# Inner v of a graph layer: two tiles of nodes by seven products in place of eight, and its bias added behind the attention weights

## The chip, the cores and the metric

The kernel runs on one core of a Trainium2 chip. TensorE (PE in the profile) multiplies matrices and writes PSUM; VectorE (DVE) and ScalarE (ACT) do the elementwise work and empty PSUM; GpSimd (POOL) and SyncE (SP) mostly start DMAs. The metric is the device time of one execution in microseconds.

## The reference

The input has 384 nodes of 1024 features. A layernorm is followed by a graph attention layer with 16 heads of 64, then a feed-forward network with fake quantisation, each with a residual. What matters here, with n the normalised input:

```
q, k, v = n @ wq.T + bq, n @ wk.T + bk, n @ wv.T + bv
q2, k2, v2 = q @ wiq.T + biq, k @ wik.T + bik, v @ wiv.T + biv   # "inner" projections
scores = q2 @ k2.T / 8 + mask                                    # per head, 384 x 384
out = softmax(scores) @ v2                                       # per head
x = x + out @ wo.T + bo
```

Everything in the attention layer is float32. The rows of a softmax sum to one, so a bias added to every row of v2 comes out of `softmax(scores) @ v2` unchanged.

## The kernel before, in words

The kernel goes through stages: the input's layernorm, the first projections q, k, v and inner q (22 to 159 us of the profiled span), the attention loop (159 to about 320), and the output projection with the feed-forward network.

The first projections and inner k already use a scheme of seven products in place of eight: two blocks of outputs by two halves of the columns, with sums of weights (`left_sums`, L171 to L175) and sums of activations (`right_sums`) made ahead on VectorE. `project2` runs the seven products, each four f32 matmuls of 128x128 by 192 columns (L191), and combines them while they are read out of PSUM: L205 and L215 on ScalarE, L202, L208, L219, L220 and L223 on VectorE; L212 makes one more weight sum in place.

The attention loop runs over p = 0 to 7, two heads at a time. Each p issues on TensorE: the scores of its two heads (`scores`, L639: first two tiles of rows, then the third); the transposes of the weights of p-1 (`weigh`, L669) and, at the end of p, their product with v2 (L677); some transposes for the quantised feed-forward weights (`prep`, L558, L568); and a filler, cut in sixteenths by `fill_to`, that keeps TensorE at work between these. The filler is inner k for the next two p (`project2`, at odd p) or a quarter of inner v (`inner_v(p // 2)`, at even p): 256 columns of v2 for all three tiles of nodes, each tile by eight matmuls of 256 columns (L613), emptied by one VectorE addition that adds the bias row (L619). At p = 7 the filler is the output projection (L687). Inner k and inner v write their PSUM tiles in the pool `ps_mm`, which holds two ("mm").

VectorE's part of one p: six score evictions (L645, scale, mask and row minimum), the reciprocals of the sums of exponentials (L657), six multiplications of the weights (L659), the copy of the product with v2 into `outT` (L681), the evictions of the filler, and the quantisation of one or two rows of feed-forward weights (`quantise_rows`: L515, L516, L518, L527). ScalarE takes the exponentials (L649), the copies of the transposed weights (L671) and the rest of the quantisation (L521).

The order on TensorE, SyncE and GpSimd is the order of the program, written out by hand. In the attention loop VectorE's and ScalarE's order is left to the scheduler of the framework at compile time. `tc.issue_after(ins)` adds to what a block issues on the engine of `ins` that it stands behind `ins`; `taken[-1]` is the score eviction written last so far.

All loads go through SyncE's queue in program order: the weight tiles `wt` (512 KB each, eight buffers used in turn), and the rows of the feed-forward weights (`row`, three buffers). The small inputs, among them the biases, come through GpSimd's queue at the start.

Of the kernel before, what the change touches and what calls it, by code (L numbers as in the profile page):

```python
# [12 lines left out]


# [2 lines left out]

# [6 lines left out]
F32 = mybir.dt.float32  # L24
# [4 lines left out]
ALU = mybir.AluOpType  # L29
# [3 lines left out]
P = 128  # L33
N = 384
NT = N // P
F = 1024
KC = F // P
E = 6528
EC = E // P
# [4 lines left out]
HK = KC // 2  # L44
# [13 lines left out]
def row_bcast(ap, n):  # L58
    return bass.AP(tensor=ap.tensor, offset=ap.offset, ap=[[0, P], [1, n]])
# [3 lines left out]
def gnn_ffn_kernel(ctx: ExitStack, tc: tile.TileContext, a: dict, out: bass.AP):  # L63
    nc = tc.nc

    const = ctx.enter_context(tc.tile_pool(name="const", bufs=1))
    small = ctx.enter_context(tc.tile_pool(name="small", bufs=2))
# [4 lines left out]
    ps_mm = ctx.enter_context(tc.tile_pool(name="ps_mm", bufs=2, space=PSUM))  # L72
# [11 lines left out]
    x = act.tile([P, NT, F], F32, name="actT")  # L84
    for t in range(NT):
        if t == NT - 1:
            wq_first = [load_w("wq", o) for o in range(FIRST)]
        nc.sync.dma_start(x[:, t, :], a["x"][t * P : (t + 1) * P, :])
    bias_rows = const.tile([5 * KC, P], F32)
    etw = const.tile([P, 4], F32)  # L90
    clip = const.tile([P, 2], F32)
    biv_b = const.tile([P, F], F32)


    ident = const.tile([P, P], F32)
# [2 lines left out]
    ph1_stack = ExitStack()  # L98
    ph1 = ph1_stack.enter_context(tc.tile_pool(name="ph1", bufs=2))
    edges_i = ph1.tile([EC, 3, P], I32, name="edges_i", bufs=1)  # L100
    nc.gpsimd.dma_start(bias_rows, a["biases"])
    nc.gpsimd.dma_start(etw, row_bcast(a["L0_gnn_edge_type_weights"], 4))
    nc.gpsimd.dma_start(clip[:, 0:1], row_bcast(a["L0_ffn_clip_x"], 1))
    nc.gpsimd.dma_start(clip[:, 1:2], row_bcast(a["L0_ffn_clip_down"], 1))
# [37 lines left out]

    ident_b = const.tile([P, P], BF16)
    later = ph1.tile([P, GROUP * P], F32, name="later", bufs=1)
    bias = const.tile([P, 5 * KC], F32)
    w8 = const.tile([P, 4], F32)

    def right_sums(src, pool, name, in_place=True):
# [98 lines left out]
    vT = act.tile([P, KC, N], F32, name="actT")  # L247
    with ph1_stack:
# [65 lines left out]
        pt = ps_tp.tile([P, P], F32, name="tp")  # L314
# [37 lines left out]
        wln = small.tile([P, 4], F32, name="wln")  # L352
        nc.scalar.activation(wln, wexp, AF.Ln, bias=1.0)
        pt = ps_tp.tile([P, 512], F32, name="tp")
        nc.tensor.transpose(pt[:, : 5 * KC], bias_rows, ident[: 5 * KC, : 5 * KC])
        wq_next = [load_w("wq", o) for o in (2, 3)]
        sums_next, steps = left_sums(*wq_next, ph1)
        run(steps)
        nc.vector.tensor_copy(bias, pt[:, : 5 * KC])
        x_right, steps = right_sums(xnT, ph1, "x_right", in_place=False)  # L360
        run(steps)
        q_first(0, 2)
# [2 lines left out]
        pt = ps_tp.tile([P, 3, EC], F32, name="tp")  # L365
# [7 lines left out]
        def tables():  # L373

            wpos = small.tile([P, 4], F32, name="wpos")
            nc.vector.tensor_scalar(wpos, etw, 0.0, None, op0=ALU.max)
            nc.vector.tensor_copy(ident_b, ident)
            nc.vector.tensor_scalar(later, ahead, 0.0, None, op0=ALU.is_gt)
            yield

            ty = small.tile([P, EC], F32, name="ty")
            nc.vector.tensor_scalar(ty, ed[:, 2, :], -1.0, None, op0=ALU.add)
            wrap = small.tile([P, EC], F32, name="wrap")
            nc.vector.tensor_scalar(wrap, ty, 0.0, 4.0, op0=ALU.is_lt, op1=ALU.mult)
            yield
            ty1 = small.tile([P, EC], F32, name="ty1")
            nc.vector.tensor_add(ty1, ty, wrap)
            ty2 = small.tile([P, EC], F32, name="ty2")
            nc.vector.tensor_scalar(ty2, ty1, 0.0, 3.0, op0=ALU.max, op1=ALU.min)
            yield  # L390
            off = small.tile([P, P], F32, name="off")
            nc.vector.tensor_scalar(off, ident, 0.0, NO_EDGE, op0=ALU.is_equal, op1=ALU.mult)
            wsp = small.tile([P, 4], F32, name="wsp")
            nc.vector.tensor_add(wsp, wpos, wln)
            nc.vector.tensor_scalar(w8, wsp, 1.0 / SCALE, None, op0=ALU.mult)
            yield

            for t in range(NT):
                nc.vector.scalar_tensor_tensor(
                    mask[:, t, t * P : (t + 1) * P], ident, w8[:, 3:4], off, op0=ALU.mult, op1=ALU.add  # L400
                )
            yield
            nc.gpsimd.dma_start(mask_d.rearrange("(t p m) a -> p t (m a)", t=NT, p=P), mask)

            nc.vector.tensor_scalar(value, ty2, 0.0, w8[:, 0:1], op0=ALU.is_equal, op1=ALU.mult)
            for k in range(1, 4):
                vk = small.tile([P, EC], F32, name="vk")
                nc.vector.tensor_scalar(vk, ty2, float(k), w8[:, k : k + 1], op0=ALU.is_equal, op1=ALU.mult)
                nc.vector.tensor_add(value, value, vk)
                yield  # L410
# [57 lines left out]
        for i, (name, o) in enumerate(todo[:-1]):  # L468
            (wa, wb), sums = wq_next, sums_next
            right, dst, cols = work[name]  # L470
# [8 lines left out]
            sums_next, steps = left_sums(*wq_next, turned if todo[i + 1][0] == "wik" else ph1)  # L479
# [3 lines left out]
            if name == "wv" and o >= KC - 4:  # L483
                steps = in_turn(steps, islice(q_steps, 4))
            if name == "wiq" and o == KC - 4:
                k_right, k_steps = right_sums(kT, turned, "k_right")
                steps = in_turn(steps, islice(k_steps, 4))
# [22 lines left out]
    v2 = act.tile([P, NT, F], F32, name="actT")  # L510
    outT = act.tile([P, KC, N], F32, name="actT")
# [60 lines left out]
    prep = ffn_weights()  # L572

    next(prep)
    nc.sync.dma_start(biv_b, row_bcast(a["L0_gnn_biv"], F))

    with ExitStack() as ph:
        at = ph.enter_context(tc.tile_pool(name="at", bufs=4))
        pair_p = ph.enter_context(tc.tile_pool(name="pair", bufs=2))
        ps_sc = ph.enter_context(tc.tile_pool(name="ps_sc", bufs=4, space=PSUM))  # L580

        def inner_k(p):
# [11 lines left out]
                ps_mm, "mm",  # L594
            )

        def inner_v(c):

            cs = slice(c * 256, (c + 1) * 256)
            wt = []  # L600
            for j in range(2):
                wt.append(w.tile([P, F], F32, name="wt"))
                nc.sync.dma_start(
                    wt[j].rearrange("p (k o) -> p k o", k=HK),
                    a["wiv"][j * HK : (j + 1) * HK, :, cs].rearrange("k p o -> p k o"),
                )

            def steps():
                for t in range(NT):
                    pm = ps_mm.tile([P, 256], F32, name="mm")  # L610
                    for k in range(KC):
                        k0 = k % HK * 256
                        nc.tensor.matmul(  # L613
                            pm, vT[:, k, t * P : (t + 1) * P], wt[k // HK][:, k0 : k0 + 256],
                            start=(k == 0), stop=(k == KC - 1),
                        )
                        if k < KC - 1:
                            yield
                    nc.vector.tensor_add(v2[:, t, cs], pm, biv_b[:, cs])  # L619
                    yield  # L620

            return steps()


        taken = []
# [36 lines left out]
        def weigh(p, e):  # L662

            eT = [[None] * NT for _ in range(2)]
            for m in range(NT):
                for h in range(2):
                    pt = ps_tp.tile([P, N], F32, name="tp")
                    for t in range(NT):
                        nc.tensor.transpose(pt[:, t * P : (t + 1) * P], e[h][:, t, m * P : (m + 1) * P], ident)  # L669
                    eT[h][m] = at.tile([P, N], F32, name="eTs", bufs=6)  # L670
                    nc.scalar.copy(eT[h][m], pt)  # L671
                yield
            pav = ps_sc.tile([P, N], F32, name="sc")
            for m in range(NT):
                for h in range(2):
                    c0 = (2 * p + h) * D
                    nc.tensor.matmul(  # L677
                        pav[h * D : (h + 1) * D, :], v2[:, m, c0 : c0 + D], eT[h][m],
                        start=(m == 0), stop=(m == NT - 1),
                    )  # L680
            nc.vector.tensor_copy(outT[:, p, :], pav)  # L681
            yield

        def out_group(wo, t, g, ks, pm):
# [12 lines left out]
        NP = H // 2  # L697
# [4 lines left out]
        for p in range(NP):  # L702
# [4 lines left out]
            if p == NP - 1:  # L707
                early = [(t, g, ps_mm.tile([P, 512], F32, name="mm")) for t, g in ((0, 0), (0, 1))]
                fill, n = (s for t, g, pm in early for s in out_group(wo, t, g, range(NP - 2), pm)), 2 * (NP - 2)
            elif p % 2:  # L710
                k2_next, fill = inner_k(p + 1)
                n = 7 * HK + 1
            else:
                fill, n = inner_v(p // 2), NT * KC
            if p == NP - 2:

                x = act.tile([P, NT, F], F32, name="actT")
# [126 lines left out]
        for t in range(NT):  # L844
# [7 lines left out]
            for g, (c0, width) in enumerate(groups):  # L852
                pm = open_groups.get((t, g)) if t < NT - 1 else None
                ks = [NP - 1]
                if pm is None:
                    pool, name = (ps_mm, "mm") if g < 2 else (ps_sc, "sc")
                    pm, ks = pool.tile([P, 512], F32, name=name), range(KC)
                for k in ks:
                    nc.tensor.matmul(
                        pm[:, :width], outT[:, k, t * P : (t + 1) * P], wo[k][:, c0 : c0 + width],  # L860
                        start=(k == 0), stop=(k == KC - 1),
# [9 lines left out]
    with ExitStack() as ph:  # L871
# [85 lines left out]
        for col, ic, c0, width in ((0, 0, 0, N), (1, 1, 0, N), (2, 2, 0, N // 2), (3, 2, N // 2, N // 2)):  # L957
            i0, rows = ICS[ic]
            cs = slice(c0, c0 + width)
# [118 lines left out]
```

## Time and profile before

| | |
|---|---|
| median of 3 runs | 369.69 us (369.19 to 370.16) |
| profiled execution | 369.01 us, its span 367.2 us |
| granted TensorE clock | 0.996 |
| TensorE busy | 355.4 us (97%) |
| VectorE busy | 255.4 us (70%) |
| ScalarE busy | 116.1 us (32%) |
| GpSimd busy | 73.7 us (20%) |
| HBM | 41.91 MB read, 2.21 MB written |

How the profile is read: busy times are of one execution. An f32 matmul leaves two records on TensorE; the duration of one record is longer than its distance to the next, since matmuls are pipelined, so what one costs is read from a run of them in the chain. In lines of the timeline the columns are the start (us from the start of the span), the duration, the engine, the line of the kernel, the operation, output and inputs, their shapes, and how many were merged; a bracket names the idle time before it and what ended it. In the chain in order of time the columns are start, duration and what ran. In the table by stretches they are the stretch, its length, and then for each of TensorE, its weight loads, VectorE, ScalarE and GpSimd the busy time and the number of instructions; the last three are the granted clock, the DMA share and GB/s, and an engine without work may be left out of the line as it is quoted from a view of one engine.

### The profile page before, as it was taken

Reading aid. Unit: us, or ns where it says so; the run is one execution under the profiler, and the core shown is the slowest. Engines: PE = TensorE matmul, PEld = TensorE weight load, DVE = VectorE, ACT = ScalarE, POOL = GpSimd, SP = SyncE. Lnnn points to the kernel's source line nnn. Section 1 sums busy time; section 2 is a strip of 40 time slices with the busy share of each in tenths; the row PEclk is TensorE's granted clock in tenths of the full one; section 3 lists DMA queues with packets and bytes.
Section 4 is the critical chain, followed back from the end, with each engine's and each line's share of the span. In section 5 each row is a group of like instructions: output and inputs, shape, how many; then the busy total and the mean of one; then the engine's idle time right before and its main releaser. Section 6 shows DMA issues by size and latency. Waiting matters only on the chain.

```text
span 367.2 us, 5815 instructions
## 1 busy us (share of the span) xinstructions
PE 355.4 (97%) x2094; PEld 297.4 (81%) x2094; DVE 255.4 (70%) x786; ACT 116.1 (32%) x270; POOL 73.7 (20%) x81
## 2 busy tenths in 40 slices
PE   8999999999999999999999999999999999999981
PEld 7999999999999999998877879686867445449660
DVE  5788888888889989967286855747494521099775
ACT  2252000000000003214473737454553523133730
POOL 7010354455444543340000000000000000000003
PEclk9999999999999999999999999999999999999998
DMA  7969433343333367720500620031694000000004
GB/s 230 396 218 401 151 116 114 118 136 116 114 114 117 114 203 253 222 64 2 157 20 2 207 63 20 17 139 44 206 404 160 29 0 2 0 0 1 2 1 171
DMA packets 17804, 44.50 MB, mean 121 GB/s; under 512 B 3262, under 2 KB 8400, under 8 KB 17392
## 3 DMA queue, kind: packets, MB, share of 16 engines
q1 hardware_dynamic: 15104, 39.46, 31.3%
q0 software_dynamic: 2672, 4.68, 4.3%
q8 instruction: 16, 0.26, 0.3%
q14 instruction: 12, 0.10, 0.1%
HBM read 41.91 MB, written 2.21 MB: 120 GB/s over the span
## 4 chain that ended last, share of the span: by engine, by line
PE 86%; DVE 10%; DMA 2%; issue 0%; SPq 0%; DVEq 0%
PE p L191 37%; PE mm L613 12%; PE mm L191 9%; PE sc L639 5%; PE sc L677 5%; PE tp L669 4%; PE mm L687 3%; PE sc L687 3%; PE mm L308 3%; DMA wt<-in_wq_dram 2%; DVE st L795 1%; PE mm L964 1%; DVE y L1017 1%; PE x L964 1%; DVE actT L790 1%; DVE lo L796 1%
## 5 line engine op out<-in xcount | busy, mean ns | idle before, releaser
L438 POOL DMA_INDIRECT mask_d<-value,place x51 | 58.2, 1142 | 65.9 <-DVE place L435 45.7
L191 PE MATMUL p<-actT,wt 128*128 128x192 f32 x360 | 65.9, 326 | 0.0
L191 PEld LDWEIGHTS p<-actT,wt 128*128 128x128 f32 x360 | 59.7, 190 | 0.0
L613 PE MATMUL mm<-wt,actT 128*128 128x256 f32 x192 | 45.9, 384 | 0.0
L613 PEld LDWEIGHTS mm<-wt,actT 128*128 128x128 f32 x192 | 34.9, 190 | 7.8 <-issue 2.8
L649 ACT ACTIVATE e<-s,mn 128x384 f32<-128x384 f32 x48 | 29.0, 605 | 32.3 <-DVE mn L645 32.3
L645 DVE CUSTOM_DVE_ANT_0 s<-sc,mask 128x384 f32<-128x384 f32 x48 | 24.6, 552 | 15.8 <-PE sc L639 15.8
L191 PE MATMUL p<-x_right,s 128*128 128x192 f32 x176 | 32.2, 326 | 0.0
L191 PE MATMUL p<-x_right,wt 128*128 128x192 f32 x176 | 32.2, 326 | 0.0
L876 POOL MEMSET hT<- 128x384 f32 x1 | 0.4, 417 | 152.0 <-PE sc L677 152.0
L191 PEld LDWEIGHTS p<-x_right,s 128*128 128x128 f32 x176 | 29.2, 190 | 0.0
L191 PEld LDWEIGHTS p<-x_right,wt 128*128 128x128 f32 x176 | 29.2, 190 | 0.0
L425 DVE SCALAR_TENSOR_TENSOR junk<-key_b,key,later 128x384 f32<-128x384 f32 (+3 forms) x51 | 27.5, 539 | 0.0
L671 ACT COPY eTs<-tp 128x384 f32<-128x384 f32 x48 | 20.5, 478 | 21.8 <-PE tp L669 21.7
L205 ACT COPY actT<-p 128x192 f32<-128x192 f32 x15 | 4.8, 319 | 63.7 <-PE p L191 63.7
L202 DVE SCALAR_TENSOR_TENSOR actT<-p,bias,actT 128x192 f32<-128x192 f32 x45 | 18.7, 415 | 8.6 <-PE p L191 6.3
L215 ACT ACTIVATE actT<-p,bias 128x192 f32<-128x192 f32 x15 | 6.3, 420 | 50.2 <-PE p L191 50.2
L669 PEld LDWEIGHTS tp<-ident,e 128*128 128x128 f32 x144 | 17.2, 141 | 4.5 <-issue 2.6
L639 PE MATMUL sc<-k,actT 64*128 64x384 f32 x96 | 20.1, 518 | 0.0
L669 PE MATMUL tp<-ident,e 128*128 128x128 f32 x144 | 19.7, 273 | 0.0
L191 PE MATMUL mm<-actT,wt 128*128 128x192 f32 x96 | 19.0, 330 | 0.0
L619 DVE TENSOR_TENSOR actT<-mm,biv_b 128x256 f32<-128x256 f32 x12 | 5.0, 421 | 17.9 <-PE mm L613 17.8
(228 smaller groups left out, 598.8 us busy)
## 6 DMA issues: line engine op xcount, KB each, us to landing
wt<-in_wq_dram SPq DMA_DIRECT2D x8, 512.0 KB, 11.4
wt<-in_wk_dram SPq DMA_DIRECT2D x8, 512.0 KB, 4.1
wt<-in_wv_dram SPq DMA_DIRECT2D x8, 512.0 KB, 4.1
wt<-in_wiq_dram SPq DMA_DIRECT2D x8, 512.0 KB, 3.8
wt<-in_wik_dram SPq DMA_DIRECT2D x8, 512.0 KB, 4.6
wt<-in_wiv_dram SPq DMA_DIRECT2D x8, 512.0 KB, 4.7
wt<-in_wo_dram SPq DMA_DIRECT2D x8, 512.0 KB, 6.9
actT<-in_x_dram SPq DMA_DIRECT2D x6, 512.0 KB, 4.2
```

Of the source, the lines that this page charges most:

```text
L191: nc.tensor.matmul(z, left[:, k * P : (k + 1) * P], r[:, k, :], start=(k == 0), stop=(k == HK - 1))
L202: nc.vector.scalar_tensor_tensor(dst, z, b, with_, op0=ALU.add, op1=ALU.add)
L425: nc.vector.scalar_tensor_tensor(junk[:, :left], keys[:, (c - k0) * P : (c - k0) * P + left], key[:, c : c + 1], later[:, :left], op0=ALU. ...
L438: ins = nc.gpsimd.indirect_dma_start(out=mask_d, out_offset=bass.IndirectOffsetOnAxis(ap=place[:, c : c + 1], axis=0), in_=value[:, c : c ...
L613: nc.tensor.matmul(pm, vT[:, k, t * P : (t + 1) * P], wt[k // HK][:, k0 : k0 + 256], start=(k == 0), stop=(k == KC - 1),)
L639: nc.tensor.matmul(ps[t, h], q2[hs, t * P : (t + 1) * P], k2[hs, :], start=True, stop=True)
L645: taken.append(nc.vector.tensor_tensor_reduce(s, ps[t, h], mask[:, t, :], -SCALE, 3.0e38, op0=ALU.add, op1=ALU.min, accum_out=mn[h][:, t : ...
L649: nc.scalar.activation(e[h][:, t, :], s, AF.Exp, bias=mn[h][:, t : t + 1], scale=-1.0, accum_out=sm[h][:, t : t + 1],)
L669: nc.tensor.transpose(pt[:, t * P : (t + 1) * P], e[h][:, t, m * P : (m + 1) * P], ident)
L671: nc.scalar.copy(eT[h][m], pt)
L677: nc.tensor.matmul(pav[h * D : (h + 1) * D, :], v2[:, m, c0 : c0 + D], eT[h][m], start=(m == 0), stop=(m == NT - 1),)
L687: nc.tensor.matmul(pm, outT[:, k, t * P : (t + 1) * P], wo[k][:, gs], start=(k == 0), stop=(k == KC - 1))
```

## The change

Inner v's first quarter of columns (p = 0) stays as it is but for its bias. For the other three (p = 2, 4, 6) the third tile of nodes is computed as before (`plain`), and the first two tiles by seven products of 128x128 blocks (`seven`), each four matmuls of 128 columns; two products share a PSUM tile. The sums of v, `v_left`, are made once, at p = 1, one of them in place in `vT`; the sums of the weights, `v_right`, are made at p = 1, 3 and 5 for the p that follows. The weights of a quarter are now loaded by `load_v` an iteration earlier. The bias of inner v is loaded as eight more rows of `bias_rows` and added when the weighted v2 is read out of PSUM (L681); its 512 KB broadcast `biv_b` goes. Some small tiles move to another pool.

```diff
...
     ph1_stack = ExitStack()
     ph1 = ph1_stack.enter_context(tc.tile_pool(name="ph1", bufs=2))
     edges_i = ph1.tile([EC, 3, P], I32, name="edges_i", bufs=1)
-    nc.gpsimd.dma_start(bias_rows, a["biases"])
+    nc.gpsimd.dma_start(bias_rows[: 5 * KC], a["biases"])
+    nc.gpsimd.dma_start(bias_rows[5 * KC :], a["L0_gnn_biv"].rearrange("(c p) -> c p", p=P))
     nc.gpsimd.dma_start(etw, row_bcast(a["L0_gnn_edge_type_weights"], 4))
     nc.gpsimd.dma_start(clip[:, 0:1], row_bcast(a["L0_ffn_clip_x"], 1))
     nc.gpsimd.dma_start(clip[:, 1:2], row_bcast(a["L0_ffn_clip_down"], 1))
...
     prep = ffn_weights()
 
     next(prep)
-    nc.sync.dma_start(biv_b, row_bcast(a["L0_gnn_biv"], F))
 
     with ExitStack() as ph:
         at = ph.enter_context(tc.tile_pool(name="at", bufs=4))
         pair_p = ph.enter_context(tc.tile_pool(name="pair", bufs=2))
+        vs = ph.enter_context(tc.tile_pool(name="vs", bufs=1))
         ps_sc = ph.enter_context(tc.tile_pool(name="ps_sc", bufs=4, space=PSUM))
 
         def inner_k(p):
...
                 ps_mm, "mm",
             )
 
-        def inner_v(c):
-
+        v_left = vs.tile([P, 3, HK, P], F32, name="v_left")
+
+        def v_left_sums():
+
+            a11, a12, a21, a22 = (vT[:, k0 : k0 + HK, t * P : (t + 1) * P] for t in range(2) for k0 in (0, HK))
+            s1, s2, s4 = (v_left[:, j] for j in range(3))
+            nc.vector.tensor_add(s1, a21, a22)
+            nc.vector.tensor_sub(s2, s1, a11)
+            nc.vector.tensor_sub(s4, a12, s2)
+            nc.vector.tensor_sub(a21, a11, a21)
+
+        def load_v(c):
             cs = slice(c * 256, (c + 1) * 256)
             wt = []
             for j in range(2):
...
                     wt[j].rearrange("p (k o) -> p k o", k=HK),
                     a["wiv"][j * HK : (j + 1) * HK, :, cs].rearrange("k p o -> p k o"),
                 )
-
-            def steps():
-                for t in range(NT):
-                    pm = ps_mm.tile([P, 256], F32, name="mm")
-                    for k in range(KC):
-                        k0 = k % HK * 256
-                        nc.tensor.matmul(
-                            pm, vT[:, k, t * P : (t + 1) * P], wt[k // HK][:, k0 : k0 + 256],
-                            start=(k == 0), stop=(k == KC - 1),
-                        )
-                        if k < KC - 1:
+            return [x.rearrange("p (k o) -> p k o", k=HK) for x in wt]
+
+        def v_right_sums(wt):
+
+            b12, b21, b22 = wt[0][:, :, P:], wt[1][:, :, :P], wt[1][:, :, P:]
+            new = vs.tile([P, 4, HK, P], F32, name="v_right")
+            t1, t2, t3, t4 = (new[:, j] for j in range(4))
+            nc.vector.tensor_sub(t3, b22, b12)
+            nc.vector.tensor_sub(t1, b12, wt[0][:, :, :P])
+            nc.vector.tensor_sub(t2, b22, t1)
+            nc.vector.tensor_sub(t4, b21, t2)
+            return t1, t2, t3, t4
+
+        def inner_v(c, wt, sums=None):
+
+
+            c0 = c * 256
+
+            def plain(t):
+                pm = ps_mm.tile([P, 256], F32, name="mm")
+                for k in range(KC):
+                    nc.tensor.matmul(
+                        pm, vT[:, k, t * P : (t + 1) * P], wt[k // HK][:, k % HK, :],
+                        start=(k == 0), stop=(k == KC - 1),
+                    )
+                    if k < KC - 1:
+                        yield
+                nc.vector.tensor_copy(v2[:, t, c0 : c0 + 256], pm)
+                yield
+
+            def seven():
+                a11, a12, s3, a22 = (vT[:, k0 : k0 + HK, t * P : (t + 1) * P] for t in range(2) for k0 in (0, HK))
+                s1, s2, s4 = (v_left[:, j] for j in range(3))
+                b11, b21, b22 = wt[0][:, :, :P], wt[1][:, :, :P], wt[1][:, :, P:]
+                t1, t2, t3, t4 = sums
+                (a1, a2), (b1, b2) = (
+                    (v2[:, t, c0 : c0 + P], v2[:, t, c0 + P : c0 + 2 * P]) for t in range(2)
+                )
+
+                def products(*factors):
+
+                    z = ps_mm.tile([P, 2, P], F32, name="mm")
+                    for j, (left, right) in enumerate(factors):
+                        for k in range(HK):
+                            nc.tensor.matmul(
+                                z[:, j, :], left[:, k, :], right[:, k, :], start=(k == 0), stop=(k == HK - 1)
+                            )
                             yield
-                    nc.vector.tensor_add(v2[:, t, cs], pm, biv_b[:, cs])
-                    yield
-
-            return steps()
+                    return [z[:, j, :] for j in range(2)]
+
+                z1, z2 = yield from products((a11, b11), (s2, t2))
+                nc.scalar.copy(a1, z1)
+                nc.vector.tensor_add(b1, z2, a1)
+                z1, z2 = yield from products((a12, b21), (s1, t1))
+                nc.vector.tensor_add(a1, z1, a1)
+                nc.scalar.copy(b2, z2)
+                nc.vector.tensor_add(a2, z2, b1)
+                z1, z2 = yield from products((s3, t3), (s4, b22))
+                nc.vector.tensor_add(b1, z1, b1)
+                nc.vector.tensor_add(b2, b2, b1)
+                nc.vector.tensor_add(a2, z2, a2)
+                z1, _ = yield from products((a22, t4))
+                nc.vector.tensor_add(b1, z1, b1)
+                yield
+
+            if sums is None:
+                return (s for t in range(NT) for s in plain(t))
+            return chain(plain(NT - 1), seven())
 
 
         taken = []
...
                         pav[h * D : (h + 1) * D, :], v2[:, m, c0 : c0 + D], eT[h][m],
                         start=(m == 0), stop=(m == NT - 1),
                     )
-            nc.vector.tensor_copy(outT[:, p, :], pav)
+
+            nc.vector.tensor_scalar(outT[:, p, :], pav, bias[:, 5 * KC + p : 5 * KC + p + 1], None, op0=ALU.add)
             yield
 
         def out_group(wo, t, g, ks, pm):
...
                 k2_next, fill = inner_k(p + 1)
                 n = 7 * HK + 1
             else:
-                fill, n = inner_v(p // 2), NT * KC
+                fill = inner_v(p // 2, *(v_next if p else (load_v(0),)))
+                n = 7 * HK + 1 + KC if p else NT * KC
+            if p % 2 and p < NP - 1:
+                wt = load_v(p // 2 + 1)
+
+                with tc.issue_after(taken[-1]):
+                    if p == 1:
+                        v_left_sums()
+                    v_next = wt, v_right_sums(wt)
             if p == NP - 2:
 
                 x = act.tile([P, NT, F], F32, name="actT")
...
```

## The prediction

> **What bounds the kernel now.** I read the page first: the shares of busy time and the chain that ended last.
>
> ```profile
> PE 355.4 (97%) x2094; PEld 297.4 (81%) x2094; DVE 255.4 (70%) x786; ACT 116.1 (32%) x270; POOL 73.7 (20%) x81
> PE 86%; DVE 10%; DMA 2%; issue 0%; SPq 0%; DVEq 0%
> ```
>
> TensorE (PE) sets the end. A mean over the span doesn't say so for the edited stage, so the second view is TensorE's busy time by stretches, here p=0, p=1, p=2, p=3 of the attention loop:
>
> ```profile
> 165.00:182.00 17.00, 17.00 (x97) 1.00 0.29 89
> 182.00:198.00 16.00, 15.39 (x102) 1.00 0.05 12
> 198.00:217.00 19.00, 19.00 (x112) 1.00 0.40 131
> 217.00:234.00 17.00, 17.00 (x112) 1.00 0.04 11
> ```
>
> TensorE (second number) fills every stretch but p=1, where 0.61 us are lost. So matmul time taken away comes off the end, and a wait given to TensorE goes onto it. The third view is the timeline of VectorE (DVE) and TensorE around that 0.61 us:
>
> ```profile
> 182.92 0.55 DVE L645 CUSTOM_DVE_ANT_0 s<-sc,mask 128x384 f32<-128x384 f32 x1
> ...
> 183.40 1.22 DVE L515 TENSOR_REDUCE wmx<-row 128x1 f32<-128x1024 f32 x1
> 184.53 0.23 DVE L657 RECIPROCAL rs<-sm 128x3 f32<-128x3 f32 x2
> 184.68 0.12 DVE L516 TENSOR_SCALAR w_scale<-wmx 128x1 f32<-128x1 f32 x1
> 184.73 2.07 DVE L659 TENSOR_SCALAR e<-e,rs 128x384 f32<-128x384 f32 x6
> 186.71 0.15 DVE L518 RECIPROCAL wrs<-w_scale 128x1 f32<-128x1 f32 x1
> 186.79 0.54 DVE L645 CUSTOM_DVE_ANT_0 s<-sc,mask 128x384 f32<-128x384 f32 x1
> ...
> 189.29 0.35 DVE L208 TENSOR_TENSOR k<-mm,k 128x192 f32<-128x192 f32 x1
> ```
> ```profile
> 188.27 0.82 PE L191 MATMUL mm<-actT,wt 128*128 128x192 f32 x4
> 189.69 0.59 PE L191 MATMUL mm<-actT,s 128*128 128x192 f32 x2 [0.61 <-DVE k L208]
> ```
>
> From 183.40, the end of the last score eviction of p=0 (L645), VectorE works without a gap to the end of L208 at 189.64. L208 empties the PSUM tile of inner k's second product; there are two such tiles ("mm"), so the fourth product at 189.69 has to wait for it. TensorE is bound by VectorE at this one place.
>
> **Matmuls removed and added.** An f32 matmul leaves two records. In the chain in order of time:
>
> ```profile
> 13.80 3.13 PE mm L308 x28
> 206.58 1.73 PE mm L613 x8
> ```
>
> So 216 ns a record at 256 columns (1.73/8) and 112 ns at 128 (3.13/28). L308 too loads a fresh 128x128 weight for each record (mean 192 ns, overlapped), as the seven products will. Each changed chunk loses 16 matmuls of 256 columns (32 x 0.2163 = 6.92 us) and gains 28 of 128 (56 x 0.1118 = 6.26 us): -0.66 us, and three chunks make **-1.98 us**. The arithmetic falls by an eighth, the time by under a tenth, because the narrow form costs 0.873 ns a column against 0.845.
>
> The Trainium skill (TensorE: Matmul & The Clock Gate, "Back-to-back issue gap") speaks against narrow matmuls: with a weight load for each, bf16 matmuls of 128 columns go every 81 ns, 25 ns over what the columns take. By that my estimate would be 168 x 20 ns = 3.4 us more, a loss of 1.4 in place of the gain. L308 is the same shape and type as the new matmuls and shows no such surcharge, so the row decides.
>
> **Sums added on VectorE.** Each is a 128x512 f32 tensor_tensor, as L171 to L175 are: L173 starts at 209.59, L175 at 210.20 and the next at 210.81, so 0.61 us each. p=1 gets four left and four right sums (8 x 0.61 = 4.88 us), p=3 and p=5 four right sums each (2.44 us).
>
> Where they stand decides the case. VectorE's order isn't written by hand in this stage. The block only says that they go behind the last score eviction traced so far, which at p=1 is the L645 at 182.92. L515 stands under the same order, is traced later still, and runs at once, ahead of the reciprocals whose sums aren't there yet. Next, the six L659 go ahead of L518, which is traced later; and L518 goes ahead of four L645 whose scores are complete at 185.9. So the order takes, of what is ready, what is traced first. The sums are traced before L515, before the new p's L645 and before L208. Their inputs are there: vT was free when p=0's last matmul of this kind ended at 181.4, and the weights are asked for behind inner k's at 148.85, as soon as the tiles of the last inner-q weights come free at about 159. I put them ahead of the four L645 and of L208.
>
> - p=1: VectorE has no gap before L208, so it ends at 189.64 + 4.88 = 194.52; the fourth product waits as much longer: **+4.88 us**. Queued behind the sums are the L645, the exponentials of ScalarE that need them, and L208; TensorE waits for the last.
> - p=3: L208 ends at 223.38 after a 0.70 us gap at 220.1 (a cast waiting for ScalarE), which takes up part: 223.38 + 2.44 - 0.70 = 225.12, where the fourth product started at 224.57: **+0.6 us**.
> - p=5: 257.58 + 1.74 = 259.32 against 258.17: **+1.2 us**.
>
> Bounds: nothing, if the sums fall behind L208; 4.88 + 2.44 - 1.19 + 2.44 - 0.59 = 8.0 us, if no gap takes any up (slacks from L208's end to the fourth product: 1.19 and 0.59). Nothing gives the time back: TensorE is full in the stretches that follow.
>
> **Evictions in the new chunks.** The three evictions of a chunk (L619, 0.42 us each) become one copy, seven adds of 128 columns and two ScalarE copies. Nearest row: L208, 0.35 us at 192 columns. A pair of products shares one of the two "mm" tiles, and it must be empty when the pair after the next starts: the time for that is the pair between, 16 x 0.112 = 1.8 us, and a set of transposes (0.66). It can run out at p=2 and p=4, where L171 holds VectorE for up to 1.7 us waiting for its weights, with the adds behind it. So from 0 to 1.7 us each (no gain: L619 held nobody up), 3.4 together; I take 0.3, since VectorE is idle for over 3 us ahead of the last L619 of a chunk.
>
> **Moves of DMAs.** Three pairs of weight loads pass one small row load each on SP's queue; that row is read an iteration later, and the loads come earlier than now. At p=3 the new pair goes out behind inner k's at 203.89 and takes some 5 us, and its sums are due at 217; at p=5 it is 237.5 and 251, so no sum waits for a landing. The 512 KB broadcast of the bias goes; nobody waited for it. GpSimd issues one more small DMA (0.54 us, as L103): the edges land at 4.94 + 7.3 + 0.54 = 12.8 and are first read at 15.43. If that cover went, it would cost 0.5. The eight additions on outT replace copies (L681, 0.54 us) one for one: 0 ± 0.05 for the last, the one that TensorE waits for. One sum: 0.
>
> **Sum.** -1.98 + 4.88 + 0.6 + 1.2 + 0.3 = +5.0. The profiled execution took 369.01 us (span 367.2, 1.8 around it), giving 374.0; it is 0.7 below the median, 369.69, so the runs should show **374.7**.
>
> **Rivals.**
> - *Faster: the sums run behind L208.* VectorE idles 1.00, 1.08, 1.21 and 0.94 us at p=1 after L208 (4.2 us, against 4.88 wanted), so they nearly fit where nobody waits: 369.69 - 1.98 = 367.7. For it: this same scheduler has left L171 to L175 in idle time at p=2 and p=4. Against: there they ran as soon as their data landed, and so will the sums. It decides once no more than three sums (1.8 us) stand ahead of L208 at p=1: 0.17.
> - *Part of the sums ahead*, four at p=1 and little after: -1.98 + 2.44 + 0.6 = 370.8 to 373: 0.11.
> - *The gain and a small stall cancel*, within 0.3%: 0.06.
> - *The clock falls.* The new wait at p=1 is 0.61 + 4.88 = 5.5 us. By stretches, the granted clock held at 1.00 over a wait of 1.56 us (354.1 to 355.6) and until 364 after the last matmul's end at 359.7; the stretch 364 to 365 shows 0.74, the next 0.50, so it fell some 4.8 us after. A wait of 5.5 could just reach that. If TensorE came back at half speed for 2 to 6 us, 1 to 3 us more: 376 to 378: 0.13. The Trainium skill (TensorE: Matmul & The Clock Gate, "What's actually happening") puts the fall after an idle window of about 3.4 us and the return after as long a busy one; an estimate by it is 1.7 us more, and it would make this case the likelier one.
>
> The forecast itself (373 to 376) has 0.53.
>
> **Range and chances.** Some 0.3% (1.1 us) is what a measurement of this kernel can tell from no change. The range leaves out the faster case (0.17) and little else: 369.6 to 377.8, which also takes in sums that no gap shortens (-1.98 + 8.0 = +6.0, 375.7) with one stalled chunk (1.7) on top. Slower: 0.53 + 0.11 + 0.13 = 0.77; same 0.06; faster 0.17.
>
> **What would show it.** Right: at p=1 eight tensor_tensor of 128x512 between L645 and L645, a gap of about 5 us on TensorE released by L208, 0.6 and 1.2 us at p=3 and p=5, and 3.1 us for 28 records of a chunk's products. Wrong: no TensorE gap at p=1, with the sums behind L208; or records well over 112 ns; or gaps inside the chunks released by small adds.

## The result and the profile after

The changed kernel takes 378.58 us (377.97 to 380.13, 4 runs) against 369.44 us: a ratio of 1.0255, interval 1.0238 to 1.0273, or +9.1 us. The forecast was +5.0 and a time of 374.7, with a range to 377.8: slower, as measured, but too little. The profiled execution took 378.72 us, its span 376.9.

The page of the changed kernel, the lines that answer to those of before:

```profile
PE 356.9 (95%) x2166; PEld 300.9 (80%) x2166; DVE 268.2 (71%) x817; ACT 117.3 (31%) x276; POOL 73.3 (19%) x82
PE 78%; DVE 16%; DMA 3%; issue 1%; ACT 0%; SPq 0%; DVEq 0%; POOL 0%; POOLq 0%
```

TensorE's share of the chain falls from 86% to 78%, VectorE's rises from 10% to 16%, DMA's from 2% to 3%. Where that happens is seen on TensorE's timeline (the lines with an idle time of note in the attention loop, and what ran just ahead of and behind the first):

```profile
188.78 0.82 PE L191 MATMUL mm<-actT,wt 128*128 128x192 f32 x4
195.00 2.93 PE L191 MATMUL mm<-actT,s 128*128 128x192 f32 x8 [5.40 <-DVE k L208]
197.72 1.13 PE L731 MATMUL tp<-ident,e 128*128 128x128 f32 x6
...
218.87 0.94 PE L661 MATMUL mm<-v_right,actT 128*128 128x128 f32 x6 [1.51 <-DVE actT L669]
...
232.96 1.57 PE L191 MATMUL mm<-actT,s 128*128 128x192 f32 x8 [0.27 <-DVE k L208]
...
254.44 0.94 PE L661 MATMUL mm<-v_right,actT 128*128 128x128 f32 x6 [1.31 <-DVE actT L669]
...
268.24 1.57 PE L191 MATMUL mm<-actT,s 128*128 128x192 f32 x8 [0.44 <-DVE k L208]
```

Five waits, in order p=1 to p=5: at odd p for L208, at p=2 and p=4 for L669, the first small add of a chunk. The fourth product at p=1 also takes 2.93 us where it took 1.57, and the transposes behind it 1.13 where they took 0.82. The stretches there say why (clock: third number from the end):

```profile
193.00:194.00 1.00, 0.00 (x0) 1.00 0.00 0
194.00:195.00 1.00, 0.00 (x1) 0.96 0.12 11
195.00:196.00 1.00, 1.00 (x3) 0.50 0.56 169
196.00:197.00 1.00, 1.00 (x5) 0.50 0.00 0
197.00:198.00 1.00, 1.00 (x5) 0.50 0.00 0
198.00:199.00 1.00, 1.00 (x8) 0.83 0.00 0
```

TensorE comes back from the wait at half clock. VectorE's timeline shows the order that caused it, from the last score eviction of p=0 (now L707) to L208:

```profile
183.44 0.55 DVE L707 CUSTOM_DVE_ANT_0 s<-sc,mask 128x384 f32<-128x384 f32 x1
...
183.91 0.69 DVE L603 TENSOR_TENSOR v_left<-actT 128x512 f32<-128x512 f32 x1
...
184.60 0.66 DVE L624 TENSOR_TENSOR v_right<-wt 128x512 f32<-128x512 f32 x1
...
186.25 0.66 DVE L604 TENSOR_TENSOR v_left<-v_left,actT 128x512 f32<-128x512 f32 x1
186.83 1.07 DVE L721 TENSOR_SCALAR e<-e,rs 128x384 f32<-128x384 f32 x3
187.82 0.68 DVE L605 TENSOR_TENSOR v_left<-actT,v_left 128x512 f32<-128x512 f32 x1
188.42 0.68 DVE L606 TENSOR_TENSOR actT<-actT 128x512 f32<-128x512 f32 x1
189.03 0.69 DVE L625 TENSOR_TENSOR v_right<-wt 128x512 f32<-128x512 f32 x1
...
190.76 0.68 DVE L626 TENSOR_TENSOR v_right<-wt,v_right 128x512 f32<-128x512 f32 x1
...
191.42 0.55 DVE L707 CUSTOM_DVE_ANT_0 s<-sc,mask 128x384 f32<-128x384 f32 x1
...
191.89 0.69 DVE L627 TENSOR_TENSOR v_right<-wt,v_right 128x512 f32<-128x512 f32 x1
...
194.59 0.35 DVE L208 TENSOR_TENSOR k<-mm,k 128x192 f32<-128x192 f32 x1
```

All eight sums stand between the two, without a gap, seven of them ahead of the next score eviction at 191.42. How long each p is, from the first filler matmul of one p to that of the next, gives the account:

| p | before | after | difference | forecast |
|---|---|---|---|---|
| 1 | 17.10 | 23.53 | +6.43 | +4.88 |
| 2 | 18.55 | 19.56 | +1.01 | -0.56 |
| 3 | 16.23 | 16.84 | +0.61 | +0.6 |
| 4 | 17.54 | 18.45 | +0.91 | -0.56 |
| 5 | 16.28 | 17.05 | +0.77 | +1.2 |
| 6 | 17.15 | 16.49 | -0.66 | -0.56 |

(For an even p the forecast is the products' gain, -0.66, and a third of the 0.3 for evictions.) The six make +9.07 us. The two profiled executions differ by 9.7 us: 0.51 of that lies ahead of p=1 (its first filler matmul starts at 182.74 against 182.23) and 0.1 behind p=6. The medians differ by 9.1.

### The profile page after: what moved, and what is told of

It reads as the page before. It is cut to its first block, busy times and chain, and to the rows that moved or that the text cites. A ratio compares the mean times of both kernels' runs of the same rounds, so it can differ in the third digit from the quotient of the medians.

```text
span 376.9 us, 6009 instructions
## 1 busy us (share of the span) xinstructions
PE 356.9 (95%) x2166; PEld 300.9 (80%) x2166; DVE 268.2 (71%) x817; ACT 117.3 (31%) x276; POOL 73.3 (19%) x82
## 4 chain that ended last, share of the span: by engine, by line
PE 78%; DVE 16%; DMA 3%; issue 1%; ACT 0%; SPq 0%; DVEq 0%; POOL 0%; POOLq 0%
PE p L191 36%; PE mm L191 7%; PE mm L638 5%; PE sc L701 3%; PE sc L739 3%; PE sc L750 3%; PE mm L750 3%; DMA wt<-in_wik_dram 3%; PE mm L661 3%; PE tp L731 3%; PE mm L308 3%; DVE s L707 2%; PE tp L316 2%; DVE e L721 2%; DVE st L866 1%
## 5 line engine op out<-in xcount | busy, mean ns | idle before, releaser
L438 POOL DMA_INDIRECT mask_d<-value,place x51 | 57.4, 1125 | 68.4 <-DVE place L435 47.0
L707 DVE CUSTOM_DVE_ANT_0 s<-sc,mask 128x384 f32<-128x384 f32 x48 | 24.6, 552 | 16.1 <-PE sc L701 16.1
L638 PE MATMUL mm<-wt,actT 128*128 128x256 f32 x96 | 23.2, 388 | 0.0
L638 PEld LDWEIGHTS mm<-wt,actT 128*128 128x128 f32 x96 | 17.5, 190 | 5.9 <-issue 2.2
L739 PE MATMUL sc<-eTs,actT 128*64 128x384 f32 x96 | 17.2, 495 | 0.0
```

Of the source, the lines that this page charges most:

```text
L438: ins = nc.gpsimd.indirect_dma_start(out=mask_d, out_offset=bass.IndirectOffsetOnAxis(ap=place[:, c : c + 1], axis=0), in_=value[:, c : c ...
L638: nc.tensor.matmul(pm, vT[:, k, t * P : (t + 1) * P], wt[k // HK][:, k % HK, :], start=(k == 0), stop=(k == KC - 1),)
L707: taken.append(nc.vector.tensor_tensor_reduce(s, ps[t, h], mask[:, t, :], -SCALE, 3.0e38, op0=ALU.add, op1=ALU.min, accum_out=mn[h][:, t : ...
L739: nc.tensor.matmul(pav[h * D : (h + 1) * D, :], v2[:, m, c0 : c0 + D], eT[h][m], start=(m == 0), stop=(m == NT - 1),)
```

## The experiments

Theory A is the forecast's mechanism, the sums ahead of L208 on VectorE, with the two things that the trace added: the clock that falls with the long wait, and L171, which waits for its weights ahead of the small adds. Rival B: the narrow products and their many evictions through two PSUM tiles cost the time. Rival C: the bias part does.

**The bias part alone.** Inner v stays at eight products, loaded at even p, and none of the sums is made:

```diff
-                fill = inner_v(p // 2, *(v_next if p else (load_v(0),)))
-                n = 7 * HK + 1 + KC if p else NT * KC
-            if p % 2 and p < NP - 1:
-                wt = load_v(p // 2 + 1)
...
+                fill, n = inner_v(p // 2, load_v(p // 2)), NT * KC
...
```

> The bias part alone: biv rides with the other bias rows and is added where the weighted v2 is read out; inner v stays at eight products. Theory A (the order on VectorE: the sums stand ahead of L208, and TensorE's clock falls after the long wait) puts nothing on this part: 369.4, within 0.7. Rival C (the bias part costs: one more GpSimd DMA at the start, the addition of 0.6 us in place of the copy of 0.54 on the path at the end): 370 to 371.

369.61 us against 369.58: 0.9997 (0.9985 to 1.001). The bias part costs nothing that these runs can tell (the interval is half a microsecond to either side); rival C is out.

**The sums alone.**

```diff
-                fill = inner_v(p // 2, *(v_next if p else (load_v(0),)))
-                n = 7 * HK + 1 + KC if p else NT * KC
+                fill, n = inner_v(p // 2, v_next[0] if p else load_v(0)), NT * KC
...
-            nc.vector.tensor_sub(a21, a11, a21)
+            nc.vector.tensor_sub(s1, a11, a21)
```

> The eight left and right sums of p=1 and the four of p=3 and p=5 are made where the changed kernel makes them (the last left sum goes to a place of its own), and the loads stand where it has them, but inner v stays at eight matmuls a tile and uses none of the sums. Theory A: 4.8 us of wait at p=1, 1.6 us of half clock behind it, 0.6 and 0.8 us at p=3 and p=5, nothing at p=2 and p=4 for lack of small adds: 369.4 + 7.8 = 377.2. Rival B (the small products and their many evictions through two PSUM tiles cost the time): within 1 us of 369.4.

377.84 us: 1.0217 (1.0191 to 1.0242), +8.3. Adding sixteen sums to an engine that is idle for three tenths of the time costs nearly as much as the whole change. L208 is waited for as in the changed kernel (5.4 us at p=1), and p=2 and p=4 wait for nothing and are as long as before (18.54 and 17.54 us), though L171 waits 2.23 and 1.82 us for its weights there: no small adds stand behind it. The half clock lasted twice as long in this profile as in the changed kernel's: p=1 took 24.82 us in place of 23.53. That accounts for the 1.2 us by which the profiled execution (378.44) stands above 377.2.

**The products alone.**

```diff
-                s1, s2, s4 = (v_left[:, j] for j in range(3))
+                s1, s2, s4 = a12, a22, a11
...
-                t1, t2, t3, t4 = sums
+                t1 = t2 = t3 = t4 = wt[0][:, :, P:]
...
```

> The seven products and their evictions as in the changed kernel, but without the sums: the products take blocks of v and of the weights as they are, so v2 isn't inner v here. Theory A: three chunks at -0.66 us by 112 ns a record, no wait for L208, and the waits for the first small add at p=2 and p=4 (1.9 and 1.5 us, behind L171's wait for its weights): 369.4 - 2.0 + 3.4 = 370.8. Rival B: 375 or more.

370.39 us: 1.003 (1.0011 to 1.005), +0.8. The products cost no 5 us; against the gain of 2 us, their two waits (1.34 and 0.80 us of idle for the first small add) come out a little above zero. p=1, 3 and 5 are as long as before (17.11, 16.23 and 16.28 us). Rival B is out as the main cause; what is left of it is the wait for L669.

**The wait filled with transposes.**

```diff
+                if p == 1 and m == 9:
+                    take(fill, 2)
+                    done += 2
+                    busy = ps_tp.tile([P, P], F32, name="tp")
+                    for _ in range(30):
+                        nc.tensor.transpose(busy, ident, ident)
                 fill_to(m)
```

> The changed kernel with 30 transposes of the identity (3.3 us) ahead of the fourth product at p=1, in the 5.4 us for which TensorE waits. Theory A: the wait for L208 stays as long, but no idle stretch comes near 4.8 us, the granted clock stays at 1.00 and the eight records of the fourth product take 1.3 us in place of 2.7: 378.6 - 1.6 = 377.0. If the slow records have another cause than the clock: 378.6.

378.43 us (376.89 to 380.36): the expected 1.6 us didn't come. TensorE's timeline and stretches of this run:

```profile
189.09 3.44 PE L821 MATMUL tp<-ident 128*128 128x128 f32 x30
194.66 2.63 PE L191 MATMUL mm<-actT,s 128*128 128x192 f32 x8 [2.13 <-DVE k L208]
```
```profile
194.00:195.00 1.00, 0.34 (x2) 1.00 0.34 44
195.00:196.00 1.00, 1.00 (x5) 0.50 0.43 153
```

The idle time is cut to 2.13 us, and the clock falls all the same. Either the clock isn't set by idleness, or transposes don't count as work.

**The wait filled with multiplications.**

```diff
-                    for _ in range(30):
-                        nc.tensor.transpose(busy, ident, ident)
+                    for _ in range(14):
+                        nc.tensor.matmul(busy, ident, ident, start=True, stop=True)
```

> The changed kernel with 14 true f32 matmuls of the identity by itself (28 records of 128 columns, 3.1 us) in TensorE's wait at p=1, where 30 transposes left the clock to fall. If the gate goes by true multiplications and doesn't count transposes: the clock stays at 1.00, the fourth product takes 1.3 us in place of 2.7 and the transposes behind it 0.65 in place of 0.95: 378.6 - 1.6 = 377.0. If the clock falls for the wait itself, or for the semaphore, and not for idleness: 378.6 with 0.50 in the stretch behind it.

377.04 us (375.79 to 378.01), as expected if transposes don't count. The same two views:

```profile
194.60 1.57 PE L191 MATMUL mm<-actT,s 128*128 128x192 f32 x8 [2.28 <-DVE k L208]
```
```profile
194.00:195.00 1.00, 0.40 (x2) 1.00 0.40 72
195.00:196.00 1.00, 1.00 (x8) 1.00 0.36 125
```

The wait ends at the same time, the idle time is no shorter, the granted clock stays at 1.00, and the product is back at 1.57 us. The single runs agree: their mean granted clock is 0.992 to 0.995 in the five with multiplications (0.992 to 0.996 in the kernel before, measured beside them) and 0.985 to 0.992 in the four with transposes. The times of the two sets overlap, so the clock's price is better read in the profiles. In the changed kernel's it is 1.32 us in the product (2.72 to the next work, where before had 1.40) and 0.30 in the transposes; and p=1 is 21.91 us long with the multiplications against 23.53 in the changed kernel, 1.62 less, though the fourth product starts 12.26 us into p=1 in both.

**Three sums less ahead of L208.**

```diff
...
             prepare(2)
             next(sc)
+            if p == 0:
+                with tc.issue_after(taken[-1]):
+                    s3_sum = v_left_sums()
...
                     if p == 1:
-                        v_left_sums()
+                        s3_sum()
```

> The changed kernel with three of its eight sums at p=1 (the three left sums that need no place in v) moved behind the first score evictions of p=0, so that five stand ahead of L208; all else as it was. Theory A at 0.61 us a sum: the wait at p=1 falls from 5.4 to 3.6 us, or to 3.0 where the cast L527 falls behind L208; it is then too short for the clock to fall: 378.6 - 1.8 - 1.6 = 375.2, or 374.6. If the clock falls already after 3.4 us without a true matmul, it may fall here too: 376.8 or 376.2.

375.99 us: 1.0191 (1.0166 to 1.0215). The wait is 3.00 us, as 0.61 us a sum and the cast L527 behind L208 give. The clock fell even so:

```profile
192.00:193.00 1.00, 0.79 (x5) 0.97 0.00 0
193.00:194.00 1.00, 1.00 (x5) 0.50 0.67 173
194.00:195.00 1.00, 1.00 (x6) 0.50 0.02 7
195.00:196.00 1.00, 1.00 (x6) 0.50 0.00 0
196.00:197.00 1.00, 1.00 (x7) 0.82 0.00 0
```

It fell 0.7 us after the matmuls had begun again at 192.21, so a wait of 3.0 us was not too short for it. The mean granted clock of the five runs, 0.984 to 0.991, lies below the 0.992 to 0.996 of the kernel before in each of them. The 4.8 us that the forecast read from the tail are no threshold.

**Inner k's weights an iteration earlier.**

```diff
-                wa, wb = (load_w("wik", p + j) for j in range(2))
+                wa, wb = k_loaded
...
+            if p == 1:
+                k_loaded = [load_w("wik", 2 + j) for j in range(2)]
...
+            if p in (2, 4):
+                k_loaded = [load_w("wik", p + 2 + j) for j in range(2)]
             done = 0
```

> The changed kernel with inner k's weights for p=3 and p=5 asked for one iteration earlier on SyncE's queue, ahead of the row loads that held them up; nothing else moves. If the waits at p=2 and p=4 come from L171 standing ahead of the first small add (L669) and waiting for its weights, both go (1.9 and 1.5 us): 378.6 - 3.4 = 375.2. If they come from the two PSUM tiles or from ScalarE's copy (L668): 378.6.

375.51 us: 1.0161 (1.0141 to 1.0181), 3.1 us less than the changed kernel. No wait for L669 is left, and p=2 and p=4 are down to 17.79 and 16.88 us; L171 runs at 197.64 and 232.94, in odd p. So the waits came from L171 ahead of the small adds, and not from the two PSUM tiles or ScalarE's copy. In the changed kernel the lines were:

```profile
215.16 0.69 DVE L527 CAST wqi<-w8b 96x1024 bf16<-96x1024 int8 x1 [1.26 <-ACT w8b L521]
217.92 0.69 DVE L171 TENSOR_TENSOR s<-wt 128x512 f32<-128x512 f32 x1 [2.07 <-DMA wt<-in_wik_dram]
218.53 0.28 DVE L669 TENSOR_TENSOR actT<-mm,actT 128x128 f32<-128x128 f32 x1
```

The pair's products had ended by 214.6 and L668's copy by 216.0, but VectorE stood at L171 from 215.8 to 217.9. In the kernel before, the idle time came behind L171 to L175:

```profile
208.87 0.69 DVE L171 TENSOR_TENSOR s<-wt 128x512 f32<-128x512 f32 x1 [0.38 <-DMA wt<-in_wik_dram]
...
210.20 0.68 DVE L175 TENSOR_TENSOR wt<-wt 128x512 f32<-128x512 f32 x1
...
215.05 0.42 DVE L619 TENSOR_TENSOR actT<-mm,biv_b 128x256 f32<-128x256 f32 x1 [3.83 <-PE mm L613]
```

**The sums behind L208.** Three left sums go as in the run with three sums less; the rest are handed to `project2` as `aside`, one after each product from the second on, behind L208 of the same p:

```diff
+        def add_aside():
+            if not side:
+                return
+            step = side.pop(0)
+            if step:
+                with tc.issue_after(seconds[-1]):
+                    step()
...
-                ps_mm, "mm",
+                ps_mm, "mm", add_aside,
...
-        nc.vector.tensor_add(b1, z, a1)
+        seconds.append(nc.vector.tensor_add(b1, z, a1).ins)
...
```

> The changed kernel with the sums elsewhere: three left sums behind the first four score evictions of p=0, the last left sum and all right sums behind L208 of p=1, 3 and 5, where VectorE has gaps; the loads as in the changed kernel. Theory A: the wait at p=1 falls back to about 0.6 us, the clock stays up, p=3 and p=5 wait for nothing: 378.6 - 4.8 - 1.6 - 1.4 = 370.8, with the waits at p=2 and p=4 left. Rival B: no change at p=1 other than a shift of the wait to the later products, 376 or more.

371.49 us: 1.0068 (1.0042 to 1.0094), 7.1 less than the changed kernel. The wait at p=1 is 0.61 us again, the clock stays up, and p=3 and p=5 wait for nothing. The waits for the first small add are left (1.52 and 0.81 us).

**Both.**

> Both: the sums behind L208 and inner k's weights asked for an iteration earlier. Theory A: every added wait is gone and the gain of the narrow products is left, three times 0.66 us: 369.4 - 2.0 = 367.4, faster than the kernel before by 0.5%. Rival B: no faster than the kernel before.

367.66 us (367.24 to 368.19) against 369.25: 0.9954 (0.9939 to 0.9968), the only version that beats the kernel before. TensorE has one wait of note, the 0.61 us at p=1 that it had before:

```profile
182.00:200.00 18.00, 17.39 (x112) 1.00 0.08 29
200.00:220.00 20.00, 19.91 (x151) 1.00 0.39 124
220.00:240.00 20.00, 20.00 (x125) 1.00 0.17 45
```

By the same measure as in the table above, its p=2, 4 and 6 are 17.79, 16.87 and 16.48 us long: -0.76, -0.67 and -0.67 against before.

## Why the prediction was wrong

The sign and the main mechanism held; two terms of the sum were too small: the clock, put at nothing, and the evictions in the new chunks, put at 0.3 us.

- *The products*: -1.98 forecast, -2.10 in the last kernel. 112 ns a record held with fresh weights each, and the surcharge worked out from the Trainium skill's bf16 figure (TensorE: Matmul & The Clock Gate, "Back-to-back issue gap") didn't appear. (The 20 ns a record in that estimate were not derived; with the 25 ns named beside it, it would have been 4.2 us.)
- *The order on VectorE*: right. The sums ran ahead of L208 at every odd p, and the wait at p=1 grew by 4.79 us, for 4.88. p=3 cost 0.61 for 0.6; p=5 0.77 for 1.2, since a reduction (L515, 0.43 us to the next start) that ran right ahead of L208 before now runs behind it, at 268.11 against 267.84.
- *The clock*: wrong step. It stood in the sum at nothing and among the rivals at 0.13, since the tail had shown the fall 4.8 us after the last matmul. It fell in all four profiles with eight sums at p=1 and no multiplications put into the wait, and in the one with five, from 2.9 to 5.7 us after the last true matmul. In the changed kernel it cost 1.64 us (p=1's +6.43 less the 4.79). The estimate from the Trainium skill's rule, 1.7 us, was the better one; the trace of before had no wait in mid-kernel long enough to test it. What it showed was that 1.56 us kept the clock and that the tail had lost it after 4.8 us, less than the 5.5 forecast for the wait; read so, the fall belonged in the sum.
- *Evictions in the new chunks*: wrong size, and the larger fault. "I take 0.3, since VectorE is idle for over 3 us": measured 1.77 at p=2 and 1.58 at p=4 (+1.01 and +0.91, less the gains of 0.76 and 0.67), 3.35 in all, the upper bound of 3.4. The idle time that the forecast meant (3.83 us up to 215.05 in the kernel before) lay behind L171 to L175 and began 11.9 us into p=2. The first small add is due 9.8 us into it, when L668's copy is done, and in the changed kernel VectorE stood in L171's wait then, with the adds behind it in its order. L171 waited in the kernel before too (0.38 and 1.67 us), where no TensorE work hung on it.
- *Moves of DMAs*: counted at nothing, and it may have fed that wait. I asked if the sums would wait for the moved loads, and not what the loads do to those ahead of them. From the issue of inner k's pair to L171 it was 4.98 and 5.37 us before and 6.70 and 6.68 in the changed kernel, where inner v's pair goes out right behind it. The other runs spread more widely: 5.68 and 6.10 with the bias part alone, whose loads go out as before, and 5.47 to 7.22 in the six others that move them and leave inner k's where they are. So the move adds about 1 us on average, and that sharing the DMA engines is the cause isn't shown. The rest of this step held (the bias: nothing).

The rival "faster" counted nothing for the waits in the new chunks either: with its order alone, the sums behind L208, the time was 371.5. The 367.7 that it named came only with the weights early as well.

## What to carry to other kernels

A saving on the engine that bounds the kernel is worth only what the preparations leave of it: before a sum on an idle engine is counted at nothing, find which instruction it goes ahead of in that engine's order, and who waits for that one. Idle time spent inside a wait is not cover, since what stands behind the wait can't use it. A stall of TensorE that comes near 3 us (the shortest wait without matmuls or transposes that lost the clock here was 3.00) has to be priced with the half clock behind it.

## What the runs showed of the hardware

The stretches at half clock have two lengths. From the granted clocks (a stretch of 1 us at 0.83 holds 0.34 us at half): 0.08 + 3 + 0.34 = 3.42 us in the changed kernel, 0.06 + 3 + 0.36 = 3.42 with five sums, 3 + 0.42 = 3.42 with the transposes; with the sums alone, and with inner k's weights early (0.84 + 5 + 0.98 = 6.82), it is twice that:

```profile
193.00:194.00 1.00, 0.00 (x0) 0.95 0.00 0
...
200.00:201.00 1.00, 1.00 (x5) 0.64 0.00 0
```

that is 0.10 + 6 + 0.72 = 6.82 us. The lengths agree with the Trainium skill (TensorE: Matmul & The Clock Gate, "What's actually happening"), which has the clock set by activity in windows of 3413 ns that run freely.

The same section lets the clock fall after an idle window. By these runs it need not be wholly idle, if a window ends where the clock falls. With five sums the last true matmul ended at 189.22 and the next began at 192.21, and the clock fell at 192.94: the 3.41 us up to there hold 0.7 us of matmuls. With inner k's weights early it fell at 192.16, 2.9 us after the last matmul, and the 3.41 us up to there hold 0.5 us. The windows themselves aren't seen here, so how much work keeps the clock stays open.

The 30 transposes kept TensorE busy in the profile and did not keep its clock. The same page ("Part 4: PE-mode transpose") says that the transpose mode doesn't count as busy in the same way; the pair of runs with 30 transposes and with 14 multiplications agrees, at 0.50 and 1.00.
